# Two mixture-of-experts layers: an expert slot's rows loaded by feature quarters and turned by VectorE instead of TensorE

## The chip, the cores and the metric

The kernel runs on one core of a Trainium2 chip. The metric is the device time of one execution in microseconds (us); the median of several executions is given. PE is TensorE, ACT is ScalarE, DVE is VectorE, POOL is GpSimd and SP is SyncE, which here only issues DMAs. All arithmetic is fp32 unless a type is named.

## The reference

The input x has 2708 rows (nodes, or tokens) of 256 features, and adj is a 2708 x 2708 matrix of 0 and 1. Two layers follow each other, each an attention over the graph and then a mixture of eight experts:

```python
# layer 0 (norm() is a layer norm without weights)
x = x + elu(softmax(where(adj > 0, q @ k.T / 16, -9e15)) @ v)   # q, k, v from norm(x)
t = norm(x)
p, e = top_k(softmax(t @ Wr + br), 2);  w = p / p.sum()          # two experts of eight
x = x + sum over the two of  w * (gelu((norm(t) * ln_g[e] + ln_b[e]) @ W1[e] + b1[e]) @ W2[e] + b2[e])
# layer 1
H = norm(x) @ W_fc + b_fc
x = x + softmax(where(adj > 0, s_src + s_dst + b_att, -1e9)) @ H
t = norm(x)
x = x + sum over the best two of  p * (gelu(t @ W1[e] + b1[e]) @ W2[e] + b2[e])
```

W1 is 256 x 1024 in layer 0 and 256 x 512 in layer 1, for each expert; W2 is the other way round.

## The kernel before

**Stages.** `layer0_attention` runs first, then `experts0.run`, `layer1_attention`, `experts1.run`, and a last loop adds the two results of every token (L1589 to L1608). SP's order is written out by hand in the whole kernel; POOL follows a scheduler except in the first group of layer 1's attention. In layer 1's attention and experts the orders of PE, ACT and DVE are written out too (L942, L1399); in layer 0 a scheduler sets them.

**Routing.** As soon as a tile of 128 tokens is through its attention, `Experts.route` (L1093) norms it, finds each token's two best experts, and writes the token's row twice, once per expert, into a DRAM table `disp` (L1197, an indirect DMA from POOL). A row has 258 words: 256 features, the token's index (word 256) and its weight (word 257). The rows of one expert lie together, so 128 of them that follow each other are a chunk for one expert. `other_rows` and `behind_written` tell the framework which reads and writes of `disp` touch different rows and which must be waited for. Routing of the last tiles still goes on, step by step (`line.step`), during the first slots of the experts.

**Slots.** The expert stage works on chunks of 128 rows, called slots. There are always 45 (`OFTEN`) and up to 50 (`SLOTS`); those after the 45th stand in conditional blocks. `place` computes which chunk and which expert a slot has. The first 24 slots of layer 0 and 20 of layer 1 (`FULL_AFTER`) are placed early, the others after the last tile is routed; `pad` then writes empty rows behind each expert's last.

- `fetch_weights(s)` (L1356) loads a slot's weights by an indirect DMA from POOL into one of four ring buffers. Slots s and s + 4 use the same buffer, and the load is skipped by the hardware's bounds check where the expert stays the same. A full load is 2.2 MB in layer 0 and 1.2 MB in layer 1.
- `fetch_rows(s)` (L1373) loads a slot's 128 x 258 words by one DMA from SP into one of six buffers `xg`. Index and weight lie in the same buffer as the features.
- Both are called for slot s + 3 (`AHEAD`) while slot s is worked on, from `fetch` (L1501).

For each slot, `slot` (L1489) does the following:

- `turned` (L1410): PE turns the two halves of `xg` (128 rows x 128 features each) into PSUM (`tp`, L1414). Layer 0 then applies the expert's norm weights with two DVE instructions that read PSUM (L1418), and layer 1 copies the result with ACT (L1424). The result `xe` holds features on partitions.
- `up` (L1427): products of W1 with `xe` (`mm`, L1441), and gelu on ACT into `hT` (L1449). It also computes `bias2`, b2 times the row weight: on DVE in layer 0 (L1432), on ACT in layer 1 (L1434). An fp32 product is two passes in the profile.
- `down` (L1454), called one slot later: products of `hT` with W2 (`acc`, L1457), then `y` = acc x weight + `bias2` on DVE (L1463), then an indirect DMA from POOL that adds `y` to the tokens' rows (layer 0, L1476) or writes it (layer 1, L1469). The index for that DMA is read from `xg`.

In layer 0, `turned(s)` is called at the start of slot s. In layer 1, `turned(s + 1)` is called between `up(s)` and `down(s - 1)`.

PSUM has two banks each for `mm`, `tp` and `acc` in the expert stage, and two for `misc`.

Of the kernel before, what the change touches and what calls it, by code (L numbers as in the profile page):

```python
# [9 lines left out]
F32 = mybir.dt.float32  # L10
I32 = mybir.dt.int32
# [5 lines left out]
ALU = mybir.AluOpType  # L17
# [3 lines left out]
P = 128  # L21
N = 2708
D = 256
# [72 lines left out]
OFTEN = SURE + 2  # L96
AHEAD = 3
DROW = D + 2
FAR = 1 << 20
# [4 lines left out]
def adj_ffn_kernel(ctx: ExitStack, tc: tile.TileContext, a: dict, out: bass.AP):  # L104
# [154 lines left out]
    def normed(dst, src, mean, factor):  # L259
        return nc.vector.tensor_scalar(dst, src, mean, factor, op0=ALU.subtract, op1=ALU.mult)  # L260

    def to_columns(dst, src, r):
# [82 lines left out]
    def layer0_attention(line):  # L345
        with ExitStack() as scope, ExitStack() as until_last:
# [276 lines left out]
            def evict(b, accs, total):  # L623
                for j, t in enumerate(BLOCKS[b][2]):
                    raw = rows.tile([P, VALUES + 1], F32, name="raw", bufs=6)
                    (nc.scalar.copy if j % 2 else nc.vector.tensor_copy)(
                        raw[: ROWS[t], : D + 1], accs[j][: ROWS[t]]
                    )
                    line.add(finish(t, raw, total))

# [397 lines left out]
    class Experts:  # L1028
        def __init__(self, layer, hidden, packed_weights, w_gate, gate_bias, own_norm, xd, disp, early):
# [6 lines left out]
            self.written = []  # L1036
            self.groups = [f"written{layer}", f"late{layer}", f"apart{layer}", f"after{layer}"]
            self.early = early
# [23 lines left out]
        def other_rows(self, start, late=True):  # L1062


            groups = [self.groups[0]] if late else []
            if self.begun:
                groups.append(self.groups[1])
            for group in groups:
                tc.declare_no_dep(start.ins, group=group, reason="other rows of disp")
                tc.add_to_no_dep_group(group, start.ins)  # L1070
            if late:
                self.written.append(start.ins)
# [20 lines left out]
        def route(self, t, x, logits=None):  # L1093
# [17 lines left out]
            if own_norm:  # L1111
                xt = rows.tile([P, D], F32, name="xn", bufs=4)[:r]
                normed(xt, x[:r], mean, once)
                normed(rows2[:r, 0, :D], x[:r], mean, twice)
            else:
                xt = rows2[:r, 0, :D]
                row = normed(xt, x[:r], mean, once)
            at = rows2.bitcast(I32)[:r, :, D : D + 1]
# [200 lines left out]
        def begin_steps(self):  # L1319
            yield  # L1320
            self.begun = True
            yield from self.place(0, FULL_AFTER[self.early])
            rows_ = [self.fetch_rows(s) for s in range(AHEAD)]
            self.fetched = []
            for s in range(AHEAD):
                self.fetched.append((self.fetch_weights(s), rows_[s]))
                yield
# [45 lines left out]
        def fetch_rows(self, s):  # L1373
            disp = self.disp
            xg = self.one.tile([P, DROW], F32, name="xg", bufs=RING + 2)
            at = nc.values_load(
                self.token_row[0:1, s : s + 1], min_val=0, max_val=IDLE,
                engines=(mybir.EngineType.SP,),
                skip_runtime_bounds_check_because="a chunk begins below its region's end",
            )  # L1380
            start = nc.sync.dma_start(xg, disp[bass.ds(at, P), :])
            if s < FULL_AFTER[self.early]:
                self.other_rows(start, late=False)
            if s in (0, FULL_AFTER[self.early]):
                self.behind_written(start)
            return xg

        def run(self, line):
            with (
                self.scope,  # L1390
                tc.tile_pool(name="ffn2", bufs=2, side=self.side) as two,
                tc.tile_pool(name="ps_mm", bufs=2, space=PSUM) as ps_mm,
                tc.tile_pool(name="ps_tp", bufs=2, space=PSUM) as ps_tp,
                tc.tile_pool(name="ps_acc", bufs=2, space=PSUM) as ps_acc,
            ):
                with ExitStack() as order:
                    if not self.own_norm:

                        order.enter_context(tc.manual_schedule(engines={  # L1399
                            mybir.EngineType.PE,  # L1400
                            mybir.EngineType.Activation,
                            mybir.EngineType.DVE,
                        }))
                    self.slots(two, ps_mm, ps_tp, ps_acc, line)

        def slots(self, two, ps_mm, ps_tp, ps_acc, line):
            hidden, own_norm, xd = self.hidden, self.own_norm, self.xd
            _, hc, w2, b2, b1, ln, row = self.packed_weights

            def turned(s):  # L1410
                w, xg = self.fetched[s]
                tp = ps_tp.tile([P, GROUP, P], F32, name="tp")
                for c in range(DC):
                    nc.tensor.transpose(tp[:, c, :], xg[:, c * P : (c + 1) * P], ident)  # L1414
                xe = two.tile([P, DC, P], F32, name="xe")
                if own_norm:
                    for c in range(DC):
                        nc.vector.tensor_scalar(  # L1418
                            xe[:, c, :], tp[:, c, :],
                            w[:, ln + c : ln + c + 1], w[:, ln + DC + c : ln + DC + c + 1],  # L1420
                            op0=ALU.mult, op1=ALU.add,
                        )
                else:
                    nc.scalar.copy(xe, tp[:, :DC, :])  # L1424
                return xe
# [27 lines left out]

            def down(s, w, xg, hT, bias2, then):  # L1454
                ps = ps_acc.tile([P, D], F32, name="acc")
                for f in range(hc):
# [5 lines left out]
                y = two.tile([P, D], F32, name="y", bufs=3)  # L1462
                nc.vector.scalar_tensor_tensor(  # L1463
                    y, ps, xg[:, D + 1 : D + 2], bias2, op0=ALU.mult, op1=ALU.add
                )
                at = bass.IndirectOffsetOnAxis(ap=xg.bitcast(I32)[:, D : D + 1], axis=0)
                if not own_norm:
# [21 lines left out]
            def slot(s, s1):  # L1489
                nonlocal placed, behind, xe  # L1490
                w, xg = self.fetched[s]
                if own_norm:
                    xe = turned(s)

                after = turned(1) if s == 0 and not own_norm else None
                hT, bias2 = up(w, xe, xg[:, D + 1 : D + 2])
                if s + 1 < s1 and not own_norm:
# [3 lines left out]
                def fetch(behind_add=None):  # L1501

                    for _ in range(2 if s + AHEAD < n else E):
                        if self.pads:
                            self.pads.pop(0)()
                    if s + AHEAD < SLOTS and s + AHEAD == len(self.fetched):
                        self.fetched.append((
                            self.fetch_weights(s + AHEAD, behind_add), self.fetch_rows(s + AHEAD)
                        ))

# [14 lines left out]
                line.step()  # L1525
                behind = (s, w, xg, hT, bias2)
                if s % 5 == 4 and background:
# [118 lines left out]
```

## Time and profile before

| | us |
|---|---|
| median of 3 runs (lowest, highest) | 1236.98 (1235.24, 1242.09) |
| the profiled execution | 1241.84 |
| its span, first to last instruction | 1240.1 |
| PE busy (share of the span) | 1172.7 (95%) |
| PE weight loads busy | 943.5 (76%) |
| DVE busy | 539.7 (44%) |
| ACT busy | 447.7 (36%) |
| POOL busy | 421.4 (34%) |
| layer 0, expert stage | about 500 to 838 |
| layer 1, expert stage | about 1014 to 1210 |

The profiled execution is 4.9 us above the median, and 1.7 us of it lie outside the span. Three kinds of rows are used below. A row of a group has the line, the engine, the operation, the tiles (out<-in), the shapes and the count, then the busy time in us and the mean of one in ns, then the idle time before them in us and what ended it. A row of the order of time has the start and the length in us, then the engine and the operation; a bracket gives the idle time before it and what ended that. A row of stages has for each engine the busy time and the number of instructions, then the granted clock of PE, the share of the 16 DMA engines that was busy, and GB/s.

### The profile page before, as it was taken

Reading aid. Unit: us, or ns where it says so; the run is one execution under the profiler, and the core shown is the slowest. Engines: PE = TensorE matmul, PEld = TensorE weight load, DVE = VectorE, ACT = ScalarE, POOL = GpSimd, SP = SyncE. Lnnn points to the kernel's source line nnn. Section 1 sums busy time; section 2 is a strip of 40 time slices with the busy share of each in tenths; the row PEclk is TensorE's granted clock in tenths of the full one; section 3 lists DMA queues with packets and bytes.
Section 4 is the critical chain, followed back from the end, with each engine's and each line's share of the span. In section 5 each row is a group of like instructions: output and inputs, shape, how many; then the busy total and the mean of one; then the engine's idle time right before and its main releaser. Section 6 shows DMA issues by size and latency. Waiting matters only on the chain. (4 is left out here: it accounts for less than half of the span.)

```text
span 1240.1 us, 20059 instructions
## 1 busy us (share of the span) xinstructions
PE 1172.7 (95%) x6712; PEld 943.5 (76%) x6712; DVE 539.7 (44%) x2055; ACT 447.7 (36%) x1301; POOL 421.4 (34%) x525
## 2 busy tenths in 40 slices
PE   8989999999998999999999999999999988899890
PEld 5656666666665675899999999987999977799880
DVE  5465762845456536531121112115867775211114
ACT  3222222222212222643223332223777667344440
POOL 3010020120211214343333333334735557455450
PEclk9999999999998999999999999998999999999996
DMA  9393973999887566475667845443003325544457
GB/s 203 63 182 81 172 172 112 210 247 236 179 174 175 130 176 249 146 206 150 222 204 216 287 123 175 114 107 93 1 6 139 119 66 200 168 144 142 132 180 281
DMA packets 148355, 197.83 MB, mean 160 GB/s; under 512 B 27595, under 2 KB 131748, under 8 KB 142104
## 3 DMA queue, kind: packets, MB, share of 16 engines
q1 hardware_dynamic: 120314, 110.16, 37.5%
q0 software_dynamic: 27040, 83.56, 21.3%
q10 hardware_dynamic: 894, 2.77, 0.6%
q8 instruction: 56, 0.92, 0.3%
q14 instruction: 51, 0.42, 0.1%
HBM read 263.66 MB, written 66.15 MB: 266 GB/s over the span
## 5 line engine op out<-in xcount | busy, mean ns | idle before, releaser
L1441 PEld LDWEIGHTS mm<-xe,ring 128*128 128x128 f32 x2192 | 256.2, 193 | 28.0 <-issue 14.4
L1441 PE MATMUL mm<-xe,ring 128*128 128x128 f32 x2192 | 266.7, 278 | 11.2 <-ACT xe L1424 6.7
L1457 PE MATMUL acc<-ring,hT 128*128 128x256 f32 x1096 | 260.9, 381 | 1.6 <-ACT hT L1449 1.5
L1449 ACT ACTIVATE hT<-mm,ring 128x128 f32<-128x128 f32 x548 | 156.0, 369 | 284.4 <-issue 179.4
L1463 DVE SCALAR_TENSOR_TENSOR y<-acc,xg,bias 128x256 f32<-128x256 f32 x92 | 44.5, 483 | 396.1 <-PE acc L1457 388.9
L1457 PEld LDWEIGHTS acc<-ring,hT 128*128 128x128 f32 x1096 | 198.1, 191 | 23.5 <-ACT hT L1449 2.4
L601 PEld LDWEIGHTS acc<-v,p 128*128 128x128 f32 (+1 forms) x880 | 160.0, 190 | 65.0 <-issue 40.9
L601 PE MATMUL acc<-v,p 128*128 128x257 f32 (+1 forms) x880 | 204.7, 385 | 2.3 <-DVE p L552 1.3
L537 PE MATMUL s<-g,xnT 128*128 128x512 f32 x420 | 202.7, 603 | 0.0
L1358 POOL DMA_INDIRECT ring<-L_ffn_packed,weight_row x98 | 103.5, 1056 | 194.0 <-issue 107.1
L256 POOL TENSOR_TENSOR ln_rs<-ln_rs,minus_half 128x2 f32<-128x2 f32 x88 | 65.9, 752 | 250.5 <-DVE ln_rs L252 212.6
L1197 POOL DMA_INDIRECT disp<-row,to x88 | 90.2, 1025 | 164.4 <-DVE to L1194 58.3
L549 ACT ACTIVATE p<-s 128x512 f32<-128x512 f32 x105 | 62.5, 595 | 181.1 <-PE s L537 146.4
L844 PE MATMUL acc<-parts,m 128*128 128x266 f32 x924 | 127.7, 296 | 0.0
L844 PEld LDWEIGHTS acc<-parts,m 128*128 128x128 f32 x924 | 118.3, 187 | 4.4 <-ACT raw L871 0.9
L537 PEld LDWEIGHTS s<-g,xnT 128*128 128x128 f32 x420 | 76.6, 193 | 53.4 <-issue 50.2
L552 DVE SCALAR_TENSOR_TENSOR p<-p,mT 128x512 f32<-128x512 f32 x100 | 68.4, 686 | 94.7 <-ACT p L549 94.5
L1476 POOL DMA_INDIRECT xd<-y,xg x45 | 71.4, 1586 | 77.0 <-issue 30.7
L811 ACT CAST m<-mT 128x512 fp32r<-128x512 fp8e4 (+4 forms) x168 | 72.3, 475 | 11.3 <-PE acc L844 7.7
L1469 POOL DMA_INDIRECT xd<-y,xg x47 | 46.9, 999 | 21.1 <-PE tp L1414 8.6
L403 DVE TENSOR_SCALAR m_rows<-adj 128x512 fp8e4<-128x512 int32 (+1 forms) x105 | 42.1, 432 | 2.0 <-DMA adj<-in_adj_dram 1.9
L1414 PE MATMUL tp<-ident,xg 128*128 128x128 f32 x184 | 34.9, 273 | 4.4 <-DMA xg<-disp 3.9
(252 smaller groups left out, 1081.6 us busy)
## 6 DMA issues: line engine op xcount, KB each, us to landing
adj<-in_adj_dram SPq DMA_DIRECT2D x100, 256.0 KB
L_ffn_packed<-in_L_ffn_W_dram SPq DMA_DIRECT2D x16, 1024.0 KB
xg<-disp SPq DMA_DIRECT2D x98, 129.0 KB
L_ffn_packed<-in_L_ffn_W_dram SPq DMA_DIRECT2D x16, 512.0 KB
neighbours<-mT SPq DMA_DIRECT2D x5, 1408.0 KB
mT<-neighbours SPq DMA_DIRECT2D x5, 1408.0 KB
xin<-in_x_dram SPq DMA_DIRECT2D x42, 128.0 KB
ring<-L_ffn_packed SPq DMA_DIRECT2D x4, 1154.0 KB
```

Of the source, the lines that this page charges most:

```text
L256: nc.gpsimd.tensor_tensor(rs[:r, 1], rs[:r, 0], minus_half[:r], ALU.pow)
L537: nc.tensor.matmul(ps[:kr, :nb], xnT[:, c, k0 : k0 + kr], g[:, c, :nb], start=(c == 0), stop=(c == DC - 1 and k < KEYS),)
L552: nc.vector.scalar_tensor_tensor(p, p, LARGEST, mask, op0=ALU.min, op1=ALU.mult)
L601: nc.tensor.matmul(accs[j][:r], p[keys, q0 : q0 + r], v[keys, k, :], start=(k == 0), stop=(k == NT - 1),)
L811: nc.scalar.copy(m[:, : q1 - q0], MASKS[b].of_key(mTs[b], k)[:, q0 - b * BN : q1 - b * BN],)
L844: nc.tensor.matmul(acc[:r], masks[t], parts[:, k, i], start=(k == 0 and i == 0), stop=False,)
L1197: nc.gpsimd.indirect_dma_start(disp[:], bass.IndirectOffsetOnAxis(ap=to[:r, j : j + 1], axis=0), rows2[:r, j], None,)
L1358: start = nc.gpsimd.indirect_dma_start(w, None, packed[:], bass.IndirectOffsetOnAxis(ap=self.weight_row[:, s : s + 1], axis=0), bounds_che ...
L1441: nc.tensor.matmul(ps[:, i, :], w[:, c * hidden + f * P : c * hidden + (f + 1) * P], xe[:, c, :], start=(c == 0), stop=(c == DC - 1),)
L1449: nc.scalar.activation(hT[:, f, :], ps[:, i, :], AF.Gelu, bias=w[:, b1 + f : b1 + f + 1])
L1457: nc.tensor.matmul(ps, hT[:, f, :], w[:, w2 + f * D : w2 + (f + 1) * D], start=(f == 0), stop=(f == hc - 1),)
L1476: start = nc.gpsimd.indirect_dma_start(xd[:], at, y, None, bounds_check=N - 1, oob_is_err=False, compute_op=ALU.add)
```

## The change

- A token's row is written to `disp` with its features in another order: four groups of 64, each with 32 features of the first half and the same 32 of the second (`by_quarters`, `in_chunks`).
- `fetch_rows` issues four DMAs for the features, one for each group. Each puts its 64 features of all 128 rows on 32 partitions, in 128 pieces of 256 bytes. A fifth DMA puts index and weight in a small tile `who` of its own.
- `turned` is one DVE instruction that turns blocks of 32 x 32, from SBUF to SBUF. Layer 0 then applies the norm weights out of SBUF; layer 1 uses the turned tile as it is. PE and ACT have no part in it.
- In layer 0 each turn is ordered, on DVE, behind the `y` that was issued last (`issue_after`); the first turns stand behind the copy of the last attention tile.
- Rows are asked for up to five slots ahead (`ROWS_AHEAD`), at most two slots' rows at a time; weights still three ahead. There are seven feature buffers and eight for `who`.
- The two PSUM banks of `tp` go to `mm`, which has four.
- The declarations on `disp` separate reads from writes, and the last of a slot's five loads ends the wait list.

In the order of the built program, a steady slot of layer 0 has on PE the 16 products `mm`, then the last four products `acc` of the slot before and the first four of its own. Before, these were 16 `mm`, the last six `acc` of the slot before, two turns of the next slot, and the first two `acc` of its own. SP's issues for the slots' rows are 500, for 100 sets, in place of 98 in the profiled execution.

```diff
+ROWS_AHEAD = 5
...
+    def in_chunks(x):
+        return x.rearrange("p (c g j) -> p g c j", c=DC, g=GROUP)
+
+    def by_quarters(row):
+
+        return row.rearrange("p (g c j) -> p g c j", g=GROUP, c=DC)
...
                         raw[: ROWS[t], : D + 1], accs[j][: ROWS[t]]
                     )
+                    if j == 0:
+                        experts0.issued = copied
...
-                normed(rows2[:r, 0, :D], x[:r], mean, twice)
+                normed(by_quarters(rows2[:r, 0, :D]), in_chunks(x[:r]), mean, twice)
             else:
-                xt = rows2[:r, 0, :D]
-                row = normed(xt, x[:r], mean, once)
+                row = normed(by_quarters(rows2[:r, 0, :D]), in_chunks(x[:r]), mean, once)
...
         def fetch_rows(self, s):
-            disp = self.disp
-            xg = self.one.tile([P, DROW], F32, name="xg", bufs=RING + 2)
+
+            disp, wide = self.disp, D // GROUP
+            xg = self.one.tile([P, GROUP, wide], F32, name="xg", bufs=ROWS_AHEAD + 2)
+            who = self.one.tile([P, 2], F32, name="who", bufs=ROWS_AHEAD + 3)
...
-            start = nc.sync.dma_start(xg, disp[bass.ds(at, P), :])
...
+            chunk = disp[bass.ds(at, P), :]
+            starts = [
+                nc.sync.dma_start(
+                    xg[g * QUARTER : (g + 1) * QUARTER],
+                    chunk[:, g * wide : (g + 1) * wide].rearrange("(t i) e -> i t e", t=GROUP),
+                )
+                for g in range(GROUP)
+            ]
+            starts.append(nc.sync.dma_start(who, chunk[:, D:]))
...
-                tc.tile_pool(name="ps_mm", bufs=2, space=PSUM) as ps_mm,
-                tc.tile_pool(name="ps_tp", bufs=2, space=PSUM) as ps_tp,
+                tc.tile_pool(name="ps_mm", bufs=4, space=PSUM) as ps_mm,
...
             def turned(s):
-                w, xg = self.fetched[s]
-                tp = ps_tp.tile([P, GROUP, P], F32, name="tp")
-                for c in range(DC):
-                    nc.tensor.transpose(tp[:, c, :], xg[:, c * P : (c + 1) * P], ident)
+
+                w, (xg, _) = self.weights[s], self.rows_[s]
                 xe = two.tile([P, DC, P], F32, name="xe")
+                raw = two.tile([P, DC, P], F32, name="xe_raw") if own_norm else xe
+                with tc.issue_after(self.issued.ins) if own_norm and s < OFTEN else ExitStack():
+                    nc.vector.transpose(
+                        raw.rearrange("p c (t i) -> p t c i", t=GROUP),
+                        xg.rearrange("p t (c j) -> p t c j", c=DC),
+                    )
                 if own_norm:
                     for c in range(DC):
                         nc.vector.tensor_scalar(
-                            xe[:, c, :], tp[:, c, :],
+                            xe[:, c, :], raw[:, c, :],
...
-                else:
-                    nc.scalar.copy(xe, tp[:, :DC, :])
                 return xe
...
-                nc.vector.scalar_tensor_tensor(
-                    y, ps, xg[:, D + 1 : D + 2], bias2, op0=ALU.mult, op1=ALU.add
-                )
-                at = bass.IndirectOffsetOnAxis(ap=xg.bitcast(I32)[:, D : D + 1], axis=0)
+                self.issued = nc.vector.scalar_tensor_tensor(
+                    y, ps, who[:, 1:2], bias2, op0=ALU.mult, op1=ALU.add
+                )
+                at = bass.IndirectOffsetOnAxis(ap=who.bitcast(I32)[:, 0:1], axis=0)
...
-                    if s + AHEAD < SLOTS and s + AHEAD == len(self.fetched):
-                        self.fetched.append((
-                            self.fetch_weights(s + AHEAD, behind_add), self.fetch_rows(s + AHEAD)
-                        ))
+                    if s + AHEAD < SLOTS and s + AHEAD == len(self.weights):
+                        self.weights.append(self.fetch_weights(s + AHEAD, behind_add))
+                    for _ in range(2):
+                        at = len(self.rows_)
+                        if at <= s + ROWS_AHEAD and at < (SLOTS if placed else n):
+                            self.rows_.append(self.fetch_rows(at))
```

More of the change, by code (lines that the diff above doesn't have):

```diff
@@ L625, in evict @@
                     raw = rows.tile([P, VALUES + 1], F32, name="raw", bufs=6)
-                    (nc.scalar.copy if j % 2 else nc.vector.tensor_copy)(
+                    copied = (nc.scalar.copy if j % 2 else nc.vector.tensor_copy)(
                         raw[: ROWS[t], : D + 1], accs[j][: ROWS[t]]
                     )
+                    if j == 0:
+                        experts0.issued = copied
                     line.add(finish(t, raw, total))
@@ L1036, in __init__ @@
             self.written = []
-            self.groups = [f"written{layer}", f"late{layer}", f"apart{layer}", f"after{layer}"]
+            self.groups = [f"written{layer}", f"late{layer}", f"apart{layer}", f"after{layer}", f"rows{layer}"]
             self.early = early
@@ L1062, in other_rows @@
         def other_rows(self, start, late=True):
-            groups = [self.groups[0]] if late else []
+            beside = [(self.groups[0], self.groups[0])] if late else []
             if self.begun:
[L1067 to L1070, printed above, removed]
+                reads, writes = self.groups[1], self.groups[4]
+                beside.append((reads, writes) if late else (writes, reads))
+            for other, own in beside:
+                tc.declare_no_dep(start.ins, group=other, reason="other rows of disp")
+                tc.add_to_no_dep_group(own, start.ins)
             if late:
@@ L1322, in begin_steps @@
             yield from self.place(0, FULL_AFTER[self.early])
-            rows_ = [self.fetch_rows(s) for s in range(AHEAD)]
-            self.fetched = []
+            self.rows_ = [self.fetch_rows(s) for s in range(AHEAD)]
+            self.weights = []
             for s in range(AHEAD):
-                self.fetched.append((self.fetch_weights(s), rows_[s]))
+                self.weights.append(self.fetch_weights(s))
                 yield
@@ L1380, in fetch_rows @@
             )
-            start = nc.sync.dma_start(xg, disp[bass.ds(at, P), :])
[L1382 to L1386, printed above, removed]
+            chunk = disp[bass.ds(at, P), :]
[7 more added lines that the diff above has]
+            starts.append(nc.sync.dma_start(who, chunk[:, D:]))
+            for i, start in enumerate(starts):
+                if s < FULL_AFTER[self.early]:
+                    self.other_rows(start, late=False)
+                if s in (0, FULL_AFTER[self.early]):
+                    self.behind_written(start, last=(i == GROUP))
+            return xg, who
         def run(self, line):
@@ L1403, in run, with slots @@
                         }))
-                    self.slots(two, ps_mm, ps_tp, ps_acc, line)
-        def slots(self, two, ps_mm, ps_tp, ps_acc, line):
+                    self.slots(two, ps_mm, ps_acc, line)
+        def slots(self, two, ps_mm, ps_acc, line):
             hidden, own_norm, xd = self.hidden, self.own_norm, self.xd
@@ L1452, in up, with down @@
                 return hT, bias2
-            def down(s, w, xg, hT, bias2, then):
+            def down(s, w, who, hT, bias2, then):
                 ps = ps_acc.tile([P, D], F32, name="acc")
@@ L1490, in slot @@
                 nonlocal placed, behind, xe
-                w, xg = self.fetched[s]
+                w, (_, who) = self.weights[s], self.rows_[s]
                 if own_norm:
@@ L1495, in slot @@
                 after = turned(1) if s == 0 and not own_norm else None
-                hT, bias2 = up(w, xe, xg[:, D + 1 : D + 2])
+                hT, bias2 = up(w, xe, who[:, 1:2])
                 if s + 1 < s1 and not own_norm:
@@ L1525, in slot @@
                 line.step()
-                behind = (s, w, xg, hT, bias2)
+                behind = (s, w, who, hT, bias2)
                 if s % 5 == 4 and background:
```

## The prediction

> **What bounds the kernel now.** I read the page first, then the chain of waits, then the order of time and the table of stages inside the two expert stages, last the DMA view. The page: PE busy 95% of a span of 1240.1 us, VectorE 44%, ScalarE 36%, DMA queues about 60%. So time comes off where an instruction leaves PE's stream, and comes on where PE waits. The edited turn is on PE:
>
> ```profile
> L1414 PE MATMUL tp<-ident,xg 128*128 128x128 f32 x184 | 34.9, 273 | 4.4 <-DMA xg<-disp 3.9
> L1418 DVE TENSOR_SCALAR xe<-tp,ring 128x128 f32<-128x128 f32 x90 | 32.7, 402 | 0.2 <-PE tp L1414 0.2
> L1424 ACT COPY xe<-tp 128x256 f32<-128x256 f32 x47 | 18.1, 386 | 8.3 <-PE tp L1414 8.3
> ```
>
> 184 turns are two for each of 92 slots: 45 in layer 0 (about 500 to 838 us), 47 in layer 1 (1014 to 1210 us). The 273 ns is latency. What a turn takes of PE's stream is read from starts, here in a steady slot of layer 0 (order of time; start, us, engine):
>
> ```profile
> 646.06 2.76 PE L1457 MATMUL acc<-ring,hT 128*128 128x256 f32 x12
> 648.65 0.38 PE L1414 MATMUL tp<-ident,xg 128*128 128x128 f32 x2
> 648.86 0.48 DVE L1463 SCALAR_TENSOR_TENSOR y<-acc,xg,bias 128x256 f32<-128x256 f32 x1 [5.96 <-PE acc L1457]
> 648.87 1.03 PE L1457 MATMUL acc<-ring,hT 128*128 128x256 f32 x4
> 649.26 0.72 DVE L1418 TENSOR_SCALAR xe<-tp,ring 128x128 f32<-128x128 f32 x2
> 649.76 3.81 PE L1441 MATMUL mm<-xe,ring 128*128 128x128 f32 x32
> ```
>
> Twelve passes of acc take 2.59 us (0.216 each), two turns 0.22, four more passes 0.89, and mm starts as xe arrives. The slot repeats every 7.34 us with no idle PE, so the 0.22 is paid in full. In layer 1 the chain shows the same step: the sum of its two rows is 3.51, the distance from mm to mm 3.74.
>
> ```profile
> 1110.09 1.78 PE mm L1441 x16
> 1112.09 1.73 PE acc L1457 x8
> 1113.82 1.78 PE mm L1441 x16
> ```
>
> Not all of layer 1 runs so. In its first eight slots, routing still shares ScalarE with the gelus (two table loads of 1.28 each a slot), the distance is about 4.6 to 4.9, and PE waits on ScalarE's copy. Later, where the ring changes experts, DMA decides:
>
> ```profile
> 1036.81 2.05 PE L1441 MATMUL mm<-xe,ring 128*128 128x128 f32 x16 [0.75 <-ACT xe L1424]
> 1068.46 2.02 PE L1441 MATMUL mm<-xe,ring 128*128 128x128 f32 x16 [2.34 <-DMA ring<-L_ffn_packed,weight_row]
> 1072.43 0.41 PE L1414 MATMUL tp<-ident,xg 128*128 128x128 f32 x2 [1.95 <-DMA xg<-disp]
> 1148.52 2.02 PE L1441 MATMUL mm<-xe,ring 128*128 128x128 f32 x16 [0.65 <-DMA ring<-L_ffn_packed,weight_row]
> 1157.09 0.41 PE L1414 MATMUL tp<-ident,xg 128*128 128x128 f32 x2 [1.92 <-DMA xg<-disp]
> ```
>
> These two bursts (1056 to 1077, 1139 to 1158 us) cost 6.2 and 4.4 us against a pitch of 3.74. The row loads are late there because SP holds each until the scatter of the slot six earlier has read its indices from the same buffer (SP's waits: 148.6 us in 37 times).
>
> [...] The trace has 396 ns for the mask turn (L409, 128 columns of int32)[...]. [...] L1418 takes 402 ns for 128 columns out of PSUM, L1432 350 ns for 256 out of SBUF. [...] after the 1068 and 1072 waits sixteen mm took 3.00 us instead of 1.95[...].
>
> **The change part by part.**
>
> *Layer 0, turns off PE.* In the order of the changed program the tp rows are gone from PE, and a slot reads mm x16 products, acc x4 of the slot before, acc x4 of its own. VectorE reads y, turn, bias, two xe. So the turn of slot s+1 can start only when the results of s-1 are out, and mm of s+1 follows four products (eight passes, 8 x 0.216 = 1.73 us) later. The chain into that window, from the end of the last acc: y starts at 0.21 (648.86 - 648.65) and the next start is 0.40 later. The turn is not in the trace with this shape. From below: the mask turn of 160 columns took 343 ns, 96 columns more at about 1 ns is 0.44 long and some 0.36 to the next start (L409's next start is 0.07 to 0.15 before its end). From above: twice L409, 0.79 long, about 0.7 to the next start. I take 0.36, since L409 has a fixed part and a scattered output. Then bias 0.27 (350 ns less the 0.08 overlap), then xe from SBUF about 0.28. Sum: 0.21 + 0.40 + 0.36 + 0.27 + 0.28 = 1.52, that is 0.2 inside the window; the second xe ends at 1.72 and is wanted at 1.95. At the upper price it is 1.86, a stall of 0.14 a slot. The four landings for which a turn waits are five slots old and cost only the waiting itself, which y's 0.40 covers. Gain: 42 steady slots x 0.22 = 9.2 (3.3 at the upper price).
>
> *Layer 0, first three slots.* The turn of slot 2 stands behind y of slot 0, and in VectorE's order some nine routing instructions (about 3 us) lie between y and xe, against six passes of acc on PE (1.3 us). Between 0 and -5; I take -2.0.
>
> *Layer 1, steady.* VectorE's order is turn of s+1, then y of s-1, so xe is ready some 2 us early, and ScalarE's copy goes. 33 slots x 0.22 = 7.3. If rows came late, the turn would hold y, and through it the scatter and the free index buffer; they are asked for five slots (17 us) ahead and land in 4.3 (median).
>
> *Layer 1, first slots.* ScalarE bounds them, so its copy counts in full: 7 x 0.37 = 2.6, PE's turns included. Four buffers for mm in place of two change nothing here, as ScalarE is full.
>
> *Row loads on SP and in the DMA engines.* Five issues in place of one: 5 x 0.333 = 1.7 us of SP, about 2 with the registers, under 3.5 a slot. SP still waits for a scatter, now only for the small index load. At the start 15 issues (some 6 us) replace 3, 12 and 25 us before the first use. In the engines a row set today is 144 packets and 13.1% of 4 us x 16: 0.52 us of all sixteen, 58 ns a packet. Masks in 512 B packets (20 to 60 us: 7226 packets, 49.0%) cost 43 ns. The line through both gives an estimate of 36 ns for 256 B and 28 for 8 B: 512 x 36 + 128 x 28 is 22 engine-us, 1.37 us of sixteen, 0.85 more a slot. Outside the bursts this is covered: DMA share in layer 0 is about 0.55, in layer 1
>
> ```profile
> 1085.00:1120.00 35.00, 34.96 (x244) 32.68 (x243) 4.35 (x9) 17.05 (x57) 19.19 (x20) 1.00 0.45 137
> ```
>
> *The bursts.* In the first, two more sets before the weights land: the 2.34 wait grows by 1.7, but the row wait and most of the slow clock go: +0.5. In the second, five sets add 4.2 us to a stretch that is full; the last weights come at about 1161.7 where mm ran at 1159.1: -2.6. Together -2.1, between -8 and +5. The seven slots inside gain nothing else.
>
> *Free.* Rows written by quarters keep count and length (bounds -1 to +1). Two more sets (100 for 98) land past the last used slot, unseen. Nothing at the layer change or in the last 30 us moves.
>
> **Sum:** 9.2 - 2.0 + 7.3 + 2.6 - 2.1 = 15.0. The profiled execution took 1241.8 us (span 1240.1), so it would take 1226.8; it was 4.9 above the median of the three runs, so I forecast 1237.0 - 15.0 = 1222.
>
> **Rivals.** (1) *VectorE's chain becomes layer 0's bound.* With the turn at 0.7 and some waits on four semaphores in the open, the stall is 0.2 a slot and layer 0 gains nothing; layer 1's 7.8 less the 2.0 remain: 1231 to 1233. For it: 0.2 of slack rests on an unseen duration. Against: VectorE's starts overlap everywhere. (2) *Slower: short packets fill the DMA engines in layer 1.* Other traffic there is 0.45 x 3.73 - 0.52 = 1.16 us a slot, so a row set above 2.35 us (59 ns a packet over 640) makes DMA the bound. [...] Against: 43 ns at 512 B. (3) *The bursts shrink:* rows in hand well ahead remove both row waits and the slow clock, and weights land as before: 6 more, 1215. That the turns stay on PE is excluded by the order.
>
> **How the numbers follow.** A difference of about 0.5% (6.2 us) is what a measurement can tell from none. Forecast 0.62, rival 1 0.15, rival 2 0.13, rival 3 0.10. Faster 0.72, within 0.5% 0.15, slower 0.13. The range runs from rival 3 with the bursts' better bound (1211) over rival 1 to 1240 with layer 0's first slots and the bursts at their worse bounds; rival 2 is left out.
>
> **What would show it.** Right: no tp on PE, mm to mm 7.12 in layer 0 and 3.51 in layer 1, a turn of 0.4 to 0.5 us, no PE wait on xg, longer waits on the ring in the second burst. Wrong: PE waiting on xe in each slot of layer 0 (rival 1); DMA share near 1 through layer 1 and waits on rows or ring outside the bursts (rival 2).

## The result, and the profile after

The changed kernel takes 1228.4 us (median of six executions, 1226.3 to 1232.3) against 1241.7 for the kernel before in the same comparison: ratio 0.9915, 95% interval 0.9897 to 0.9934. Measured again beside later kernels, it was 0.9924 (0.9910 to 0.9939). The profiled execution took 1228.5 us, its span is 1226.7. The kernels below were measured in three groups, each on another chip (numbers 1 to 4; the control and 5 to 7; 8 to 11). The kernel before had medians of 1248.1, 1238.4 and 1239.6 us in them, so ratios are compared and not times. The changed kernel itself stands in the second group alone, so a step from it to a kernel of another group takes for granted that the ratio carries over; where an event of the trace shows the step as well, it is given. The clock times of two traces can differ by up to 2 us before anything in them does: SP's last issue ahead of the experts' rows comes at 465.5 to 467.6 us.

I read the changed kernel in the order in which I read the one before. The groups of the page first: no `tp` is left on PE, and the turn is a VectorE instruction of 0.43 us (line, operation, tiles, count, then busy us and mean ns):

```profile
L1436 DVE STREAM_TRANSPOSE xe_raw<-xg 128x256 f32<-128x256 f32 x45 | 19.4, 433 | 0.0
```

A steady slot of layer 0, in order of time (start us, duration us, engine, line, what it writes):

```profile
644.56 3.62 PE L1479 MATMUL acc<-ring,hT 128*128 128x256 f32 x16
646.49 0.48 DVE L1485 SCALAR_TENSOR_TENSOR y<-acc,who,bias 128x256 f32<-128x256 f32 x1 [5.44 <-PE acc L1479]
646.89 0.43 DVE L1436 STREAM_TRANSPOSE xe_raw<-xg 128x256 f32<-128x256 f32 x1
647.25 0.31 DVE L1454 TENSOR_SCALAR bias<-ring,who 128x256 f32<-128x256 f32 x1
647.48 0.59 DVE L1442 TENSOR_SCALAR xe<-xe_raw,ring 128x128 f32<-128x128 f32 x2
648.02 3.73 PE L1463 MATMUL mm<-xe,ring 128*128 128x128 f32 x32
```

The sixteen `acc` stand without a gap, and `mm` starts 3.46 us after the first of them. The chain on VectorE runs y, turn, bias, xe at distances of 0.40, 0.36 and 0.23, and nobody waits. Slot to slot it is 7.03 us, where it was 7.34. In layer 1 the same order of time shows 3.51 from `mm` to `mm`, where it was 3.74:

```profile
1107.15 1.95 PE L1463 MATMUL mm<-xe,ring 128*128 128x128 f32 x16
1108.94 1.89 PE L1479 MATMUL acc<-ring,hT 128*128 128x256 f32 x8
1110.66 1.95 PE L1463 MATMUL mm<-xe,ring 128*128 128x128 f32 x16
```

At the two changes of experts in layer 1, PE's rows with a wait are now these, in order of time:

```profile
1056.42 2.05 PE L1463 MATMUL mm<-xe,ring 128*128 128x128 f32 x16 [0.68 <-DVE xe L1436]
1064.90 2.02 PE L1463 MATMUL mm<-xe,ring 128*128 128x128 f32 x16 [1.19 <-DVE xe L1436]
...
1137.70 3.17 PE L1463 MATMUL mm<-xe,ring 128*128 128x128 f32 x16 [2.28 <-DMA ring<-L_ffn_packed,weight_row]
```

The second of these waits is put down to weights in the control below (1.34 us). So far the steps hold. The new thing is seen only when the whole of PE's waits is read from 440 us on: a wait of 8.8 us at the end of layer 0's attention, on the masked `p_last`. In order of time:

```profile
497.57 0.35 DVE L1454 TENSOR_SCALAR bias<-ring,who 128x256 f32<-128x256 f32 x1 [12.97 <-DMA who<-disp]
...
498.53 2.20 PE L609 MATMUL acc<-v,p_last 128*128 128x257 f32 x4 [8.78 <-DVE p_last L560]
```

That `bias` is slot 0's `bias2`. The scheduler had put it among the attention's last instructions on VectorE, in both kernels. Before, it ran as soon as its turn came:

```profile
484.65 0.35 DVE L1432 TENSOR_SCALAR bias<-ring,xg 128x256 f32<-128x256 f32 x1
```

After, its factor comes in the separate small load `who`. VectorE stands for 13 us, the last masks of the attention stand behind it, and PE stands behind them. After the wait PE is slow as well: granted clock 0.83 in the stretch from 480 to 520 us (1.00 before), and sixteen `mm` took 3.64 us instead of 1.95. These rows of stages are of the changed kernel, then of the kernel before:

```profile
480.00:520.00 40.00, 30.11 (x149) 18.46 (x148) 14.67 (x70) 7.42 (x20) 6.76 (x11) 0.83 0.69 247
480.00:520.00 40.00, 38.56 (x236) 27.04 (x234) 22.73 (x103) 17.18 (x46) 15.79 (x23) 1.00 0.71 267
```

The spans of the two profiled executions differ by 13.4 us. Cut at marks that both traces have, they give this account (us; minus is a gain):

| stretch | measured | forecast |
|---|---|---|
| up to slot 4's results in layer 0 | +15.7 | +2.0 |
| layer 0, slots 5 to 44 | -11.8 | -9.2 (slots 3 to 44) |
| last results of layer 0 to layer 1's attention | -4.3 | 0 |
| layer 1's attention and first slots | -2.3 | -2.6 |
| the two bursts, slots in them included | -5.1 and -1.3 | -0.5 and +2.6 |
| layer 1, 25 steady slots | -5.8 | -7.3 (33 slots) |
| last two slots and the end | +1.4 | 0 |

A sum near the forecast's 15.0 came from parts that were not: up to layer 1's attention the change gave 0.4 instead of 7.2, and from there on 13.0 instead of 7.8. The table is of one execution of each kernel.

### The profile page after: what moved, and what is told of

It is laid out like the page before. It is cut to its first block, busy times and chain, and to the rows that moved or that the text cites. A ratio compares the mean times of both kernels' runs of the same rounds, so it can differ in the third digit from the quotient of the medians.

```text
span 1226.7 us, 20985 instructions
## 1 busy us (share of the span) xinstructions
PE 1150.6 (94%) x6528; PEld 928.7 (76%) x6528; DVE 565.7 (46%) x2147; ACT 435.4 (35%) x1254; POOL 421.3 (34%) x525
## 5 line engine op out<-in xcount | busy, mean ns | idle before, releaser
L1463 PEld LDWEIGHTS mm<-xe,ring 128*128 128x128 f32 x2192 | 261.9, 195 | 23.1 <-issue 7.0
L1463 PE MATMUL mm<-xe,ring 128*128 128x128 f32 x2192 | 267.5, 279 | 12.4 <-DMA ring<-L_ffn_packed,weight_row 4.7
L1479 PE MATMUL acc<-ring,hT 128*128 128x256 f32 x1096 | 255.0, 382 | 4.8 <-ACT hT L1471 4.8
L1479 PEld LDWEIGHTS acc<-ring,hT 128*128 128x128 f32 x1096 | 201.3, 191 | 29.8 <-ACT hT L1471 6.2
L1485 DVE SCALAR_TENSOR_TENSOR y<-acc,who,bias 128x256 f32<-128x256 f32 x92 | 44.4, 483 | 345.6 <-PE acc L1479 337.6
L1498 POOL DMA_INDIRECT xd<-y,who x45 | 71.3, 1583 | 101.0 <-issue 59.2
L1491 POOL DMA_INDIRECT xd<-y,who x47 | 47.0, 999 | 22.2 <-issue 11.6
L609 PE MATMUL acc<-v,p_last 128*128 128x257 f32 (+3 forms) x88 | 27.4, 413 | 8.8 <-DVE p_last L560 8.8
```

Source lines behind the costliest of these rows:

```text
L609: nc.tensor.matmul(accs[j][:r], p[keys, q0 : q0 + r], v[keys, k, :], start=(k == 0), stop=(k == NT - 1),)
L1463: nc.tensor.matmul(ps[:, i, :], w[:, c * hidden + f * P : c * hidden + (f + 1) * P], xe[:, c, :], start=(c == 0), stop=(c == DC - 1),)
L1479: nc.tensor.matmul(ps, hT[:, f, :], w[:, w2 + f * D : w2 + (f + 1) * D], start=(f == 0), stop=(f == hc - 1),)
L1498: start = nc.gpsimd.indirect_dma_start(xd[:], at, y, None, bounds_check=N - 1, oob_is_err=False, compute_op=ALU.add)
```

## The experiments

**Theory:** layer 0's gain is spent by one late load of 1 KB at its start, and the load is late because it stands behind the weights in the DMA engines. **Rivals:** the new order of the first slots costs it; the small loads are slow by themselves; or the layer change takes back what layer 0 gains, whatever happens before.

**1. The small loads first.** In the changed kernel:

```diff
-            self.rows_ = [self.fetch_rows(s) for s in range(AHEAD)]
+            for s in range(AHEAD):
+                self.fetch_rows(s, "who")
+            self.rows_ = [self.fetch_rows(s, "rows") for s in range(AHEAD)]
```

> The changed kernel with one edit: at the start of a layer's slots the three small loads of indices and factors (who) are issued ahead of the twelve quarter loads, in place of one behind each set of four. Theory A, the late who: slot 0's bias waits 12.97 us on VectorE for who, the last attention masks stand behind it, TensorE waits 8.8 us and then runs at a low clock, and slot 4 begins 17 us later than in the kernel before. Then VectorE's wait on who falls below 1 us, TensorE's on p_last below 1 us, slot 4's products begin near 535 us instead of 549.7, and the time is 1215 to 1219 us. Rival B, the layer change takes it back: the stall goes but layer 1's attention begins no sooner, 1226 to 1229 us. Rival C, the new order of the first slots is what costs: the 8.8 goes, but slots 2 to 4 still lose 6 us against the kernel before, 1220 to 1223 us.

Ratio 0.9862 (0.9834 to 0.9891). VectorE no longer waits on `who`, so `who` it was and not the weights that `bias` also reads. Another wait took its place, in PE's list of waits (us in total, times, longest):

```profile
PE mm L1476 <- DMA xg<-disp: 6.2, 1, 6.2
```

The first products began at 506.6 us; before it was 501.0, in the changed kernel 511.8. From there to slot 4's results it took 49.2 us, with PE's order the same as in the changed kernel, which took 49.9; before it was 45.0. SP's rows say why the rows were late: the twelve quarter loads took from 478.4 to 505.4 to issue. Layer 1's attention began 5.7 us sooner than in the changed kernel, so the layer change took nothing back. Half of theory A holds, its 1215 us does not: the next late load stood behind the first. And rival C keeps a share: 4 us are still lost in the first slots.

**2. Layer 1 alone, first try.** Layer 0 as before (whole rows, turns on PE, two `mm` banks), layer 1 as changed:

```diff
+            if self.own_norm:
+                return self.whole_rows(s)
```

> Only layer 1 has the change (quarter loads, VectorE's turn, rows five ahead, four mm banks); layer 0 is as in the kernel before: whole rows, turns on TensorE, two banks. Theory A, layer 1 alone makes the gain and layer 0's gain was spent at its own start: 1228 to 1230 us, 12 to 13 us below the kernel before, with layer 1's expert stage as long as in the changed kernel. Rival, both layers share the gain as forecast (layer 1 7.8, layer 0 7.2): 1233 to 1235 us.

Ratio 0.9969 (0.9952 to 0.9986). This was not a clean cut: the scheduler had given PE another order in layer 0's first slots, and from the first products to slot 4's results it took 50.8 us instead of 45.0, with no late load in sight. PE waits three times there, 4.0 us together, and none of it is put down to a load of rows or weights. So another order can cost 5.7 us there, and the kernel was done again as number 8. The ratio is worth about 4 us, where the expectations had 12 to 13 and 7 to 8.

**3. Rows three slots ahead instead of five.**

```diff
-ROWS_AHEAD = 5
+ROWS_AHEAD = 3
```

> The changed kernel with rows asked for three slots ahead instead of five. Theory A, the lead is what shrank layer 1's bursts (first one 5.6 us shorter): without it TensorE waits for rows again at the two changes of experts, 4 to 7 us back, 1232 to 1236 us; steady pitch stays 3.51 and 7.03. Rival, the bursts shrank because a slot is shorter or the row loads no longer wait for a scatter, not by the lead: 1227 to 1229 us.

The constant also sets the number of buffers: five for features and six for `who`, instead of seven and eight. Ratio 0.9973 (0.9956 to 0.9990), 0.5 to 0.6% (6 to 7 us) above the changed kernel, at the upper end of theory A's 4 to 7. The pitches stay. One row of the first burst carries it:

```profile
1077.96 3.69 PE L1463 MATMUL mm<-xe,ring 128*128 128x128 f32 x16 [8.82 <-DVE xe L1436]
```

The turn waits 11.3 us for rows, and with it PE for 8.8. Without the lead and its buffers most of the change's gain is gone.

**4. Two banks for `mm` instead of four.**

```diff
-                tc.tile_pool(name="ps_mm", bufs=4, space=PSUM) as ps_mm,
+                tc.tile_pool(name="ps_mm", bufs=2, space=PSUM) as ps_mm,
```

> The changed kernel with two buffers for mm in place of four, as in the kernel before. Theory A, the 0.09 us a slot that layer 0 gained beyond the 0.22 of the turns comes from the banks: pitch 7.10 to 7.12 instead of 7.03, 3 to 4 us more, 1231 to 1233 us. Rival, it comes from leaving the turns out of the stream (weight loads and the handover around them): pitch 7.03, and the time moves only by what the first slots do, 1225 to 1230 us.

Ratio 0.9961 (0.9948 to 0.9973). Neither expectation had it right: 27 of the 40 slots after the first ones take 7.24 us, and the rest 7.03 or near it. In a slot of 7.24, in order of time:

```profile
650.07 1.05 POOL L1368 DMA_INDIRECT ring<-L_ffn_packed,weight_row  x1 [4.30 <-issue]
650.10 0.32 DVE L1454 TENSOR_SCALAR bias<-ring,who 128x256 f32<-128x256 f32 x1
650.33 0.82 DVE L1442 TENSOR_SCALAR xe<-xe_raw,ring 128x128 f32<-128x128 f32 x2
650.87 3.95 PE L1463 MATMUL mm<-xe,ring 128*128 128x128 f32 x32
```

The two `xe` take 0.82 instead of 0.59, and the second ends at 651.15, just behind the end of GpSimd's issue of the ring load at 651.12. Alone it lasts 0.57 instead of 0.34. PE has begun `mm` on the first half and stands inside it for the second: 32 `mm` take 3.95 instead of 3.73. In the changed kernel (the slot at 644.56 above) the ring issue begins 0.24 us behind y's start instead of 0.73, and ends in time. Number 10 tests this.

**5. The small loads first, and weights behind rows.** Beside the edit of number 1, in layer 0 the weights of slots 1 to 3 wait for the rows of the first three slots:

```diff
-                self.weights.append(self.fetch_weights(s))
+                self.weights.append(
+                    self.fetch_weights(s, self.last_rows if self.own_norm and s else None)
+                )
```

> The changed kernel with the small loads who first, as in the first experiment, and in layer 0 also the weights of slots 1 to 3 asked for only when the rows of the first three slots have landed. There the wait of 12.97 us on who had given way to one of 6.2 us on xg, since twelve quarter loads took 27 us to issue behind weights of 2.2 MB a slot. Theory A, the weights in front are why the small loads are late: the twelve quarter loads are issued in 8 to 12 us, neither wait is left, the first products begin at 500 to 502 us (before 501.0, changed 511.8, first experiment 506.6), slot 4 near 534, and the ratio to the kernel before is 0.980 to 0.984. Rival, the small loads are slow by themselves (lanes, 8-byte packets): the wait stays at 4 us or more, ratio 0.986 as in the first experiment. Third, the late weights become the wait: TensorE waits on the ring for slots 1 to 3 and the ratio is 0.987 or more.

Ratio 0.9781 (0.9763 to 0.9799), better than theory A's 0.980 to 0.984. The quarter loads are issued in 9.6 us, the first products begin at 501.3, PE waits neither for `p_last` nor for rows, and VectorE waits 1.1 us once for slot 1's weights. Slot 4's results come at 542.1, where they came at 546.0 in the kernel before and at 561.8 in the changed one. Two things are in this. The wait accounts for the first products (511.8 to 501.3, 10.5 us). From there to slot 4 it takes 40.8 us instead of 49.9, and that has another source: with the added dependence the scheduler put the last tiles' routing among the attention's products, and PE's first two slots hold nothing else. The edit did not ask for that.

**6. Layer 0 alone.** Layer 0 as changed, layer 1 as before.

```diff
+            if not self.own_norm:
+                return self.whole_rows(s)
```

> Only layer 0 has the change; layer 1 has whole rows, turns on TensorE, ScalarE's copy and two mm banks, as before. Theory A, from the ledger of the two traces (13.0 us gained from slot 4 to the end of layer 0's slots, 16.9 lost up to slot 4, 4.3 taken back at the layer change): 0 to 1 us of gain, ratio 0.999 to 1.0. Rival, from the times of the layer-1-only kernel (ratio 0.9969 where the whole change has 0.9915): layer 0 makes the greater part, ratio 0.994 to 0.996.

Ratio 1.0010 (0.9998 to 1.0021): the change gains nothing in layer 0, with the wait of 8.7 us on `p_last` in the trace. That fits the account of the traces: 0.4 us for everything up to layer 1's attention.

**7. The lead alone.** The kernel before, with its rows asked for five slots ahead:

```diff
-            xg = self.one.tile([P, DROW], F32, name="xg", bufs=RING + 2)
+            xg = self.one.tile([P, DROW], F32, name="xg", bufs=ROWS_AHEAD + 2)
...
+                    for _ in range(2):
+                        at = len(self.rows_)
+                        if at <= s + ROWS_AHEAD and at < (SLOTS if placed else n):
+                            self.rows_.append(self.fetch_rows(at))
```

> The kernel before with one part of the change alone: whole rows in one load each, turned on TensorE, but asked for five slots ahead with seven buffers. Theory A, the lead takes away both row waits at the changes of experts in layer 1 and the low clock behind them: 4 to 6 us less, ratio 0.995 to 0.997, no wait of TensorE on xg there. Rival, the lead alone does nothing, as SP still waits for a scatter's reading of the same buffer: ratio 0.999 to 1.001.

Ratio 0.9985 (0.9970 to 0.9999), some 2 us. The row waits go, as theory A said, but the gain is smaller than it said: at the first change of experts PE now waits for weights twice, 1.28 and 0.81 us, one of them here:

```profile
1067.95 2.02 PE L1442 MATMUL mm<-xe,ring 128*128 128x128 f32 x16 [1.28 <-DMA ring<-L_ffn_packed,weight_row]
```

**Control.** The changed kernel once more, beside numbers 5 to 7, no edit.

> The changed kernel itself once more, beside the others on this chip: 0.990 to 0.993 of the kernel before, as in its first measurement, the 8.8 us wait of TensorE on p_last again. If the wait is missing, it was chance.

Ratio 0.9924, and the wait of 8.8 us on `p_last` is there again. It was no chance.

**8. Layer 1 alone, again,** with layer 0 in the order of the kernel before on every engine. The edit to number 2 only restores the order in which tiles are made (`tp` ahead of `xe`, and `ps_tp` ahead of `ps_acc`).

> The change in layer 1 alone once more, now with layer 0 in exactly the order of the kernel before on every engine (in the first layer-1-only kernel TensorE's order in layer 0's first slots had come out differently, and slot 0's results came 5.4 us later than in the kernel before). Theory A: layer 1 is where the whole net gain of the change lies, ratio 0.989 to 0.993. Rival, the first layer-1-only figure was right: 0.996 to 0.998, and the parts do not add up.

Ratio 0.9943 (0.9924 to 0.9962), about 7 us: between the two expectations. In its trace layer 0's results stand within 0.1 us of the kernel before, and from the start of layer 1's attention to the last results it takes 345.1 us instead of 356.8. With number 6 this adds up to about 0.995, where the whole change has 0.992; the intervals just about allow both.

**9. Weights behind rows, and nothing else.** The second edit of number 5 without the first.

> The changed kernel with one edit of the two that the version with ratio 0.9781 has: layer 0's weights of slots 1 to 3 are asked for only when the rows of the first three slots have landed; who stays behind its four quarter loads. Theory A, the weights in front were the whole cause: no wait of TensorE on p_last, first products at 500 to 502 us, ratio 0.977 to 0.980. Rival, who has to go first as well: a wait of 3 us or more is left on p_last and the ratio is 0.981 to 0.986.

Ratio 0.9798 (0.9777 to 0.9819), median 1212.8 us as in number 5. SP's loads and PE's first products, in order of time:

```profile
475.99 2.87 SPq L1398 DMA_DIRECT2D xg<-disp  x4
479.05 0.37 SPq L1404 DMA_DIRECT2D who<-disp  x1
...
488.79 0.35 SPq L1404 DMA_DIRECT2D who<-disp  x1
...
502.84 3.36 PE L1467 MATMUL mm<-xe,ring 128*128 128x128 f32 x28 [1.10 <-ACT raw L634]
```

The fifteen loads go out in 13 us. In the changed kernel the same fifteen took 24 (GpSimd's rows first, then SP's):

```profile
474.63 1.46 POOL L1368 DMA_INDIRECT ring<-L_ffn_packed,weight_row  x1 [2.59 <-PE misc L1189]
476.39 1.22 POOL L1368 DMA_INDIRECT ring<-L_ffn_packed,weight_row  x1 [0.31 <-issue]
477.92 0.99 POOL L1368 DMA_INDIRECT ring<-L_ffn_packed,weight_row  x1 [0.30 <-issue]
...
475.13 2.93 SPq L1395 DMA_DIRECT2D xg<-disp  x4
478.26 0.40 SPq L1401 DMA_DIRECT2D who<-disp  x1
...
492.09 6.23 SPq L1395 DMA_DIRECT2D xg<-disp  x4
498.51 0.35 SPq L1401 DMA_DIRECT2D who<-disp  x1
```

There GpSimd had issued three loads of 2.2 MB at 474.6, 476.4 and 477.9 us, just ahead of `who` at 478.3, which VectorE could use at 497.6. SP then waited for earlier loads to land before it issued later ones (14.4 us in four waits). Here slot 0's weights alone go first, and the others at 494.4 and later. Slot 0's `bias` finds its `who` there without a wait:

```profile
487.52 0.32 DVE L1458 TENSOR_SCALAR bias<-ring,who 128x256 f32<-128x256 f32 x1
```

VectorE's order is another too, and this row stands some 3 us later than before. But `who`, issued at 479.05, has landed 8.5 us later at most, where it took 19.3, so the order does not explain it. The weights in front are the cause of the wait; that `who` stands behind its quarters is not. PE's order is that of number 5, so the 25 us below the kernel before are again the wait and the better order together.

**10. Two banks, and `bias` behind `xe`.** The edit to number 4:

```diff
+                    with tc.issue_after(self.turned.ins) if s < OFTEN else ExitStack():
                         nc.vector.tensor_scalar(bias2, w[:, b2:b1], factor, None, ALU.mult)
```

> The two-bank kernel with layer 0's bias queued behind the two xe on VectorE instead of between the turn and xe. With two banks 30 of 40 slots took 7.24 us instead of 7.03, and in those the second xe took 0.565 us instead of 0.341 and ended with GpSimd's issue of the ring load. Theory A, it is that stretched xe on the path: with xe 0.23 us earlier it is hidden, all slots take 7.03; and since slot 0's bias no longer stands ahead of the attention's last masks, the 8.8 us wait on p_last goes, the first products wait for rows instead (near 506 us): ratio 0.983 to 0.988 (two banks alone: 0.9961). Rival, two banks cost 0.21 by themselves: the slots stay at 7.24, and the ratio is 0.989 to 0.993.

Ratio 0.9864 (0.9841 to 0.9887), as theory A had it. All but four of the slots take 7.03 or near it, with two banks. GpSimd's issue still lies there, but the instruction that ends with it is now `bias`, for which nobody waits:

```profile
652.71 1.05 POOL L1368 DMA_INDIRECT ring<-L_ffn_packed,weight_row  x1 [3.88 <-issue]
652.85 0.60 DVE L1442 TENSOR_SCALAR xe<-xe_raw,ring 128x128 f32<-128x128 f32 x2
653.37 0.48 DVE L1455 TENSOR_SCALAR bias<-ring,who 128x256 f32<-128x256 f32 x1
653.50 3.73 PE L1464 MATMUL mm<-xe,ring 128*128 128x128 f32 x32
```

The wait on `p_last` is gone too, since slot 0's `bias` no longer stands ahead of the masks, and PE waits 7.4 us for rows instead. So the number of banks itself costs nothing in a steady slot.

**11. Number 5 with `bias` behind `xe` as well.** Both edits, as above.

> The version with ratio 0.9781 (who first, weights of slots 1 to 3 behind the rows, four banks) with layer 0's bias queued behind the two xe as well. Theory A: the few slots of 7.2 us go (five of 44), 1 us less, ratio 0.976 to 0.978, not to be told from 0.9781. Rival, bias behind xe delays the following y in the first slots: 0.979 to 0.981.

Ratio 0.9799 (0.9778 to 0.9821), median 1213.0 us: no difference from number 5, as expected.

The version to keep is number 9, one dependence more than the changed kernel, or number 5: both 1212.8 us, 2.0 and 2.2% below the kernel before. Number 5 was measured in one group with the control, 1212.8 against 1228.3.

## Why the prediction was right or wrong

The direction was right, and so was about the size (15.0 us forecast; 13.4 between the traces, about 10.5 by the ratio), but the size in part by luck: the steady slots came as forecast, the two layers as wholes did not, and their misses nearly cancelled.

- **Layer 0, turns off PE: mechanism right, size small by 0.09.** The 0.22 of the turns goes, and so does a stall inside `mm`: before, `mm` began on the first `xe` while the second was still being made, and its 32 took 3.81; now they take 3.73. The turn took 0.43 long and 0.36 to the next start, as estimated from the mask turn (0.433 us for 256 columns against 0.343 for 160 is 0.94 ns a column; L409's 128 take 0.396), `xe`, put at 0.28 by estimate, took 0.34 out of SBUF (median; 0.40 out of PSUM before), and rival 1 (VectorE's chain as the bound) did not come. Number 4 shows how near it was: a second `xe` late by 0.23 costs 0.21 a slot.
- **"At the start 15 issues (some 6 us) replace 3, 12 and 25 us before the first use": the step that failed.** It was costed at nothing. In layer 0 the issues took 24 us, not 6, and the first use was not the first turn (500.0 us before, 25 behind the loads) but slot 0's `bias`, 9 us behind them, on the same queue as the attention's masks. The trace of before shows that row at 484.65, among the masks, and I did not ask which load had to have landed for it. The first products came 10.8 us later for it. With the cause taken away (number 9) they come 9.0 us sooner; the whole change is then worth 2.0% instead of 0.8%, though half of what is won at the start (9 of 18 us up to slot 4's results) belongs to the scheduler's other order.
- **"Layer 0, first three slots", 2.0 lost: a loss, but larger and by another way.** From the first products to slot 4's results the changed kernel takes 4.9 us more than the kernel before (49.9 and 45.0). The prediction had `xe` come late, behind routing on VectorE. PE has no such wait there. It waits 3.1 us in two waits for ScalarE's `hT` (0.5 before), and it is busy 46.9 us instead of 44.4, at a granted clock of 0.93 instead of 1.00. So about half are waits in another order, and about half goes with the low clock. In number 1, with the changed kernel's order, it is 3.5 us of waits and 45.7 busy at 0.95. Other orders give other sums: number 10, behind a wait of 7.4 us, takes 46.5; number 2 takes 50.8 and number 9 40.8. Such differences come out of the scheduler, and the order of the built program would have shown them only as an order, not as a time.
- **Nothing at the layer change moves: wrong by 4.3.** From the last results to layer 1's attention it took 19.8 us before and 15.5 after. There PE runs 28 filling products (`busy(PAUSE)`), 56 passes whose results nothing reads, ahead of the first turn of layer 1's rows. Before, then after:

```profile
837.92 1.30 PE L904 MATMUL acc<-wfc,ident 128*128 128x256 f32 x3 [1.98 <-DVEq L1548]
840.02 14.19 PE L904 MATMUL acc<-wfc,ident 128*128 128x256 f32 x53 [0.81 <-issue]
854.05 0.38 PE L266 MATMUL misc<-ident,xn 128*128 128x128 f32 x2
...
841.49 12.32 PE L914 MATMUL acc<-wfc,ident 128*128 128x256 f32 x56 [1.62 <-DVEq L1572]
853.65 0.38 PE L274 MATMUL misc<-ident,xn 128*128 128x128 f32 x2
```

  The rows to be turned (`xn`) were ready at 848.2 us before and at 852.0 after, so in both it is the filling products that end last. They took 15.5 us at a granted clock of 0.87 before (840 to 860 us) and 12.3 at 1.00 after, behind 2.8 and 1.6 us in which PE stood idle: that makes up the 4.3. The kernels with layer 0 as before have 18.5 to 20.0 in all, those with the changed layer 0 15.5, but for numbers 5, 9 and 11 with 18.3 to 18.5. In the traces with 15.5 PE idles 1.6 us ahead of the filling products, in the others 2.6 to 3.1. So it goes with the order in layer 0. Around the filling products the granted clock is 0.84 to 0.93 in the kernel before and in numbers 7, 8 and 9, which idle longer, and 1.00 in the changed kernel. Whether the idle time sets the clock, no run tests.
- **Layer 1, steady: right,** 0.22 to 0.23 a slot. **First slots: the number by another way.** 2.3 gained (layer 1's attention included) against 2.6. From the start of the attention, slot 4's `mm` begins 3.8 us sooner than before, so these slots win more at first than was forecast. But slot 6's begins only 0.9 sooner, as PE then waits for the weights of slots 5 and 6, which the prediction had only at the later changes of experts:

```profile
1033.56 2.02 PE L1463 MATMUL mm<-xe,ring 128*128 128x128 f32 x16 [1.98 <-DVE hot L1199]
1039.78 3.45 PE L1463 MATMUL mm<-xe,ring 128*128 128x128 f32 x16 [2.44 <-DMA ring<-L_ffn_packed,weight_row]
```

  The profile names `hot` for the first; in the control both are put down to the weights (2.46 and 1.89 us). The kernel before waited 0.25 us for weights there.
- **The bursts: the size of one term.** I had 2.1 lost and the traces show 6.4 gained, the gain of the slots in them included. The term is the price of a row set. These lines of the DMA view are of the changed kernel from 1082.5 to 1124.7 us (13 sets of rows), then of the kernel before from 1083.5 to 1136.0 (14 sets): packets, MB, share of 16 engines.

```profile
q1 hardware_dynamic: 9360, 1.72, 23.9%
```

```profile
q1 hardware_dynamic: 2016, 1.85, 13.7%
```

  After: 0.239 x 42.2 x 16 / 13 = 12.4 engine-us a set, 0.78 us of all sixteen, where the prediction had 1.37. Before: 0.51, as taken. So a set costs 0.26 us more and not 0.85. A set has 720 packets in the view, 80 more than the prediction counted, as each of the five loads brings 16 beside its pieces. They cost 17 ns in the mean, where the line drawn through 1032 and 512 bytes gave 36 and 28. Rival 2 needed 2.35 us a set. With rows cheap, rival 3's mechanism is what happened in the first burst, in part: numbers 3 and 7 show the lead at work, worth 0.5 to 0.6% with the new turn and some 0.15% without it.
- **Not in the sum:** the last two slots, which stand in conditional blocks. There PE waits 1.78 and 0.93 us for `xe`, where it waited 0.52 twice.
- **A reading that does not hold.** The prediction has sixteen `mm` take 3.00 us instead of 1.95 behind the waits at 1068 and 1072. These waits were 2.34 and 1.95 us, with work between them; behind the first, sixteen `mm` took 2.02 us, and only behind the second 3.00. What made those sixteen slow was not shown.

## What to carry to other kernels

When a load is split, ask for each piece which instruction reads it first in the queue as built, not in the program; that reader can stand in the stage before, ahead of work that has nothing to do with it. A small load that must land early is given its place by holding back the large ones that would stand in front of it; here (number 9) 1 KB then landed within 8.5 us instead of 19.3, and in number 5 that cost one wait of 1.1 us. And when a total comes out as forecast, cut both traces at the same marks before believing it: here two misses of 6.8 and 5.2 us nearly cancelled.

## What the runs showed of the hardware

- **Small packets were cheap.** A row set in 512 pieces of 256 bytes and 128 of 8, from DRAM into SBUF, took 12.4 us of DMA-engine time, 17 ns a packet in the mean (720 packets); in 128 rows of 1032 bytes it took 8.2, 57 ns a packet (144).
- **1 KB can take 19 us to land.** `who`, issued at 478.3, was usable at 497.6, behind three loads of 2.2 MB that were issued up to 3.6 us earlier. Behind one such load (number 9) it had landed after 8.5 us at most.
- **A VectorE instruction under way when GpSimd's DMA issue ended lasted about to that end.** In the trace of number 4 the second `xe` took 0.57 us instead of 0.34 and ended at 651.15, the issue at 651.12; in that of number 10 `bias` took 0.48 instead of 0.32 and ended at 653.85, the issue at 653.76. The instructions before it within the same 1.05 us issue ran at their usual length (in number 4 `bias` 0.32, in number 10 the two `xe` 0.60). Why, the runs do not show.
- **The turn's price.** VectorE turns 128 x 256 fp32 in blocks of 32 x 32 in 0.43 us, from SBUF to SBUF (433 ns in the mean of 45 in layer 0, 435 of 47 in layer 1).
